# A cross-attention over 4096 tokens, its transfers issued by one queue in the order in which the program is written

## The chip, the cores and the metric

The kernel runs on one core of a Trainium2 chip. A core has five engines that each work through an instruction list of their own: TensorE (PE, matmuls), VectorE (DVE), ScalarE (ACT), GpSimd (POOL) and SyncE (SP). In this kernel SP does nothing but issue transfers (DMAs) from HBM to on-chip memory and back; ACT can issue them too, between its own arithmetic. The metric is the device time of one execution, in microseconds (us). Smaller is better.

## The reference

The network is a perceiver: a short sequence x (2 batches of 256 tokens, width 256) goes through twelve residual blocks, four of which attend to a long context `ctx_1024` (2 batches of 4096 tokens, width 256):

```python
x = x + _L0_xattn_ref(_layernorm(x), ctx_1024, mask, q_w, q_b, k_w, k_b, v_w, v_b)
x = x + _L0_attn_ref(_layernorm(x), w_down_q, w_down_kv, w_up_q, w_up_k, w_up_v, w_out, ...)
x = x + _L0_ffn_ref(...)
x = x + _L1_xattn_ref(_layernorm(x), ctx_1024, mask, Wq, Wk, Wv, Wo)
...
x = x + _L3_xattn_ref(_layernorm(x), ctx_1024, ctx_1024, Wq, Wk, Wv, Wp, focusing_factor)
...
```

The change is in the first block, L0_xattn, a masked softmax attention with 16 heads of 16 columns:

```python
q = split_heads(hidden @ q_w.T + q_b)       # 256 tokens a batch
k = split_heads(context @ k_w.T + k_b)      # 4096 tokens a batch
v = split_heads(context @ v_w.T + v_b)
scores = where(mask, -inf, q @ k.T / sqrt(16))
out = softmax(scores) @ v
```

One part of a later block is computed here as well, because it depends on the context alone. L3_xattn projects its keys from the context, takes absolute values and a softmax over logarithms, keeps the 11 largest of every 16 columns, and sums the products of the keys with the context. The kernel calls these keys the features, and does one batch of them during L0_xattn and the other during L1_xattn.

## The kernel before

**Units and steps.** `ContextAttention` (L805) cuts L0_xattn into 8 units, one for each of 2 batches and 4 chunks of heads (four heads in 128 partitions, 32 for each). `attend` (from L1090) is a loop over steps g = 0, 1, ...; a unit takes 16 steps (PER), so the stage has 128 first steps and some 20 more. A unit is passed over twice. In the first pass, `first_scores` (matmuls at L1257) multiplies queries by a tile of 512 keys, and DVE takes the row maxima (L1265, L1271). In the second, two steps and a whole unit later, `scores` (L1287) computes scores the other way round with the maximum already subtracted, ACT takes exp (L1296), and `weigh` (L1308) multiplies by the values. One step does one half of a key tile in each pass: 2 steps for 512 keys.

**Fills.** Between these, PE does what a planner (`plan`, from L947) has put into `fills[g]`: `project_keys` (matmuls k_ps at L1167), `project_values` (v_ps, through the helper at L242), projections of features (f_ps, L242 too), and their sums (kc_sum). Keys are projected in steps 0, 2, 5, 8, 12 and then about every fourth step; values in steps 1, 4, 6, 7, 9, 10 and so on; the sixteen halves of the features in steps 0, 3, 14, 16, 32, 33, 46, 49, 62, 65, 79, 80, 95, 97, 110 to 113 and 114. DVE's share of the features (the search for the eleven largest, L726 and L732, on the tile `fy`) is spread over the steps by the planner as well.

**How keys reach their tiles.** `project_keys(j)` works on a pair of context tiles of 512 tokens (`ctx_k`, loaded at L1149, 512 KB each). Its result in PSUM is copied by ACT into `k_dense` (L1177, two buffers, taken in turn). From there eight DMAs of 16 rows each (L1195, 32 KB each) move it into two of 14 key tiles (`xa_k`), four heads each to its own 32 partitions, and two small DMAs (L1185) put a row of the mask into each tile. Before the rows, `project_keys` issues the loads of the next pair of `ctx_k` (`load_keys_ctx`). The mask rows come from a table in HBM that the kernel writes itself at the start (L584, from `masks`, computed on DVE).

**Who issues.** Nearly everything is issued by SP. The exception is in this stage: for the first six pairs (`BY_ACT = 6`), the four rows of the pair's first tile are issued by ACT, the other four by SP (L1194, L1195). All transfers of the two queues take eight completion semaphores in turn, so a transfer's issue instruction first waits until the one eight before it has landed.

**Homes of the keys' context.** `ctx_k` has one pair of buffers (`bufs=1`, two tags). In L0_xattn there are more at the start: `SPARE = 3`, three pairs of value tiles (`xv`) that are not yet needed, which hold every second pair of context, so that two pairs can be there at a time until the sixth projection. For that the pool of value tiles is opened with the constructor of `ContextAttention` (L530 to L543).

**Values' context.** `load_values_ctx` (L1209) loads half a tile of context (`ctx_v`, 256 KB, four buffers); four are issued ahead of the loop, and each `project_values` issues one more.

**Features' context.** `Focus.load` (L752) fetches half a tile of context (`f_ctx`, 256 KB, two buffers). `Focus.start` issues the first; each projection of a half issues the next at its start (written ahead of its matmuls). `load_tokens` (L759) fetches the tokens for the sums (`f_tok`, 512 KB).

**The order of the work.** Within `context_attention` the engines in `by_program` (PE, DVE and ACT, L529) run their instructions in the order in which the Python program writes them (`tc.manual_schedule`). SP and POOL are not among them: a scheduler orders their instructions by its own estimates and may lift a transfer over others that are written before it.

**The start.** `center` and `inverse_root` (L335, L336: `rstd` on ACT, from the variance on DVE) normalise x; then queries are projected (`take_queries`), and the first pair of keys is projected ahead of them, with its rows and masks issued there. `self.beginning` is the rest of that: in step 0 it projects the second pair of keys (j = 1) ahead of the step's fills. `l0_attn` (from L1335), the next block, begins with the load of three of its weights (`L0a_wdq`, `L0a_wdkv`, `L0a_wuv`) into one tile of the pool of weights.

Of the kernel before, what the change touches and what calls it, by code (L numbers as in the profile page):

```python
# [21 lines left out]
F32 = mybir.dt.float32  # L22
# [6 lines left out]
P = 128  # L29
# [79 lines left out]
class Net:  # L109
# [52 lines left out]
    def load(self, *names, now=None):  # L162


        nc = self.nc
        t = self.weights.tile([P, 2048], F32, tag="w", name=f"w_{names[0]}")
        at, parts = 0, []
        for name in names:
            src = self.ins[name]
            n = int(np.prod(src.shape[1:]))  # L170
            letters = "abcde"[: len(src.shape) - 1]
            flat = src
            view = t[:, at : at + n]
            if len(letters) > 1:
# [343 lines left out]
    def context_attention(self, x, q_bias, k_bias, v_bias, wq, wk, values, layer, alive=None, block=None):  # L518

        tc = self.tc  # L529
        by_program = {mybir.EngineType.PE, mybir.EngineType.DVE, mybir.EngineType.Activation}  # L530
        to_values = lambda: tc.tile_pool(name="xa_v", bufs=1, reuse_waits="tile")
        with (
            tc.tile_pool(name="xa", bufs=1, reuse_waits="tile") as big,
            tc.tile_pool(name="xa_ctx", bufs=2, reuse_waits="tile") as cpool,
            to_values() if layer == 0 else nullcontext() as vpool,
        ):
            a = ContextAttention(self, layer, big, cpool, vpool, (wk, k_bias), v_bias)
            if layer == 0:
                for issue in self.postponed:
                    issue()  # L540
                a.load_keys_ctx()
                self.nc.sync.dma_start(out=self.vectors, in_=self.ins["vectors"])
                self.focus = Focus(self)  # L543
            a.wv, wo = values()
            if block is not None:
                with tc.manual_schedule(engines={mybir.EngineType.PE}), self.stage():
                    x = block(x, a.begin(3))
            with tc.manual_schedule(engines=by_program):
                return self.attend_to_context(a, x, q_bias, wq, wo, alive, nullcontext(vpool) if vpool else to_values())

    def attend_to_context(self, a, x, q_bias, wq, wo, alive, values):
# [9 lines left out]
        with (  # L561
            self.banks(mm=4, sc=2, acc=0),
            values as vpool,
            tc.tile_pool(name="xa_p", bufs=1, reuse_waits="tile") as ppool,
            tc.tile_pool(name="focus", bufs=2, reuse_waits="tile") as fpool,
        ):
            return a.attend(vpool, ppool, fpool, x, wo)
# [237 lines left out]
class ContextAttention:  # L805
# [7 lines left out]
    LAG = 2  # L813
    KEY_TILES = 14
    VALUE_TILES = 11
    BY_ACT = 6
    SPARE = 3

    def __init__(self, net, layer, big, cpool, vpool, keys, v_bias):
# [15 lines left out]
        self.spare = vpool is not None  # L835
        self.key_homes = {}
        if self.spare:
            self.vpool = vpool
            for n in range(self.SPARE):
                self.key_homes[2 * n + 1] = [self.new_values() for _ in range(2)]  # L840
# [249 lines left out]
    def attend(self, vpool, ppool, fpool, x, wo):  # L1090
# [3 lines left out]
        self.x, self.new = x, net.new_x()  # L1094
        if self.layer == 0:
            nc.gpsimd.memset(self.new[P // 2 :, ND - 1, S:], 0.0)
        for _ in range(4):
            self.load_values_ctx()
        focus.start(self.layer, fpool)
        fills = self.plan()  # L1100
        n = len(self.UNITS)

        rankings = {}
        for g in range((n + 1) * PER + LAG + 2):
            second = g - PER - LAG
            if 0 <= second < n * PER:
                self.scores(second // PER, second % PER)
            if g < n * PER:
                pair = self.first_scores(g // PER, g % PER)
            run(self.beginning)  # L1110
            if 1 <= g < n:
                self.finish_queries(g)
            if self.layer == 0:
# [5 lines left out]
                self.weigh((second - 1) // PER, (second - 1) % PER)  # L1119
            for fill in fills.get(g, ()):  # L1120
                fill()
            for kc in self.rankings.get(g, ()):
                if kc not in rankings:
                    y, _, factor = focus.chunks[kc]
                    rankings[kc] = focus.sparsify(fpool, y, factor)
                run(rankings[kc], 1)
# [5 lines left out]
                    self.finish(wo)  # L1132
            for kc in self.weighings.get(g, ()):
                run(focus.weighing[kc], 1)
        return self.new


    def load_keys_ctx(self):
        b, kc = next(self.key_loads, (None, None))
        if b is None:  # L1140
            return
        pair, homes = [], self.key_homes.pop(len(self.key_ctx), None)
        for i in range(2):
            if homes:
                flat = homes[i].rearrange("p k v -> p (k v)")[:, : ND * KC]
                ctx = flat.rearrange("p (d n) -> p d n", d=ND)
            else:
                ctx = self.cpool.tile([P, ND, KC], F32, name=f"ctx_k{i}", tag=f"ctx_k{i}", bufs=1)
            self.nc.sync.dma_start(out=ctx, in_=self.net.ins["ctxT"][b, kc + i])  # L1149
            pair.append(ctx)  # L1150
        self.key_ctx.append(pair)

    def project_keys(self, j, first, n=1):
# [25 lines left out]
            return  # L1179
        tiles = [self.key_tiles[(2 * j + i) % self.KEY_TILES] for i in range(2)]  # L1180

        def write_mask(i):
            rows = tiles[i].rearrange("(g r) n -> g r n", r=HP)
            mask = net.key_masks[self.layer, b * NKC + kc + i]
            nc.sync.dma_start(out=rows[:, DH + 1], in_=mask.unsqueeze(0).to_broadcast([NG, KC]))  # L1185

        if not self.spare or j != 2 * self.SPARE - 1:
            self.load_keys_ctx()
        for i, k in enumerate(tiles):
            if j > 0:  # L1190
                write_mask(i)
            queue = nc.scalar if self.spare and j < self.BY_ACT and i == 0 else nc.sync
            for g in range(NG):
                at = i * HR + g * DH  # L1194
                queue.dma_start(out=k[g * HP : g * HP + DH, :], in_=dense[at : at + DH, :])  # L1195
        if j == 0:
            for i in range(2):
                write_mask(i)

    def new_values(self):  # L1200
        return self.vpool.tile([P, KC // P, VW], F32, name="xv", tag="xv", bufs=self.VALUE_TILES)

    def load_values_ctx(self):
        b, kc, k2 = next(self.value_loads, (None, None, None))
# [7 lines left out]
    def project_values(self, b, kc, k2, first, n=1):  # L1212

        net, nc = self.net, self.nc
        if k2 == first == 0:
            v = self.new_values()
# [117 lines left out]

def l0_attn(net, x):  # L1335
    nc, tc = net.nc, net.tc
    wdq, wdkv, wuv = net.load("L0a_wdq", "L0a_wdkv", "L0a_wuv")
    wups = net.load("L0a_wuq", "L0a_wuk")
    wout = net.load("L0a_wout")
    g, be = net.vec("L0a_g"), net.vec("L0a_b")  # L1340
# [1469 lines left out]
```

## Time and profile before

| What | Value |
|---|---|
| Time, median of 3 runs | 2142.94 us (2139.47 to 2145.37) |
| The profiled execution: its own time | 2143.32 us |
| Its span in the trace | 2141.3 us |
| Mean granted clock of TensorE | 0.99 |
| PE / DVE / ACT busy, 0 to 24 us | 15.98 / 4.55 / 9.26 us |
| the same, 24 to 87 us (63 us; mean PEclk 0.92) | 54.04 / 42.01 / 15.63 us |
| the same, 87 to 200 us (113 us) | 111.52 / 96.58 / 76.76 us |
| the same, 200 to 620 us (420 us) | 414.93 / 338.13 / 289.51 us |
| Loads of `ctx_k` (512 KB each), whole kernel | 122 |
| Rows `xa_k<-k_dense` on SP's queue (32 KB each) | 488 |

Durations of single instructions come from the profiled execution, one run of the kernel under the hardware profiler; its own time is 2.0 us over its span. The span's rows are stretches of the trace: the busy time of each engine in the stretch, and PEclk, the clock that the throttle granted to TensorE as a share of full speed. Step 0 of the loop begins at 24.17 us and step 16 at 86.73 us; L0_xattn ends near 620 us. A line of the timeline of an engine holds start, duration, engine, line, operation, tiles and number of instructions that were put together; a bracket at its end gives the idle time ahead and what ended it. A line of the waits says which engine waited on which line, for what, and the total, the number and the longest of these waits. A line of the windows gives, for each engine, its busy time and instructions, then PEclk, the DMA engines' mean share and GB/s.

### The profile page before, as it was taken

To read this page: it belongs to the slowest core of one execution; us is meant where nothing else is said; L and a number is where in the kernel's file an instruction comes from. 1 tells how busy PE (TensorE), PEld (TensorE's weight loads), DVE (VectorE), ACT (ScalarE), POOL (GpSimd) and SP (SyncE) were. 2 spreads that over 40 slices of the span, in tenths; PEclk is the share of its full clock that TensorE was granted. 3 is DMA by queue.
4 is the path that set the end of the run, shared out by engine and by line. 5 is a ranking of instruction groups with operands and counts; after the bars stand their busy time and mean duration, and the time that the engine had idled before them with its cause. 6 is when DMAs were issued, how large, how long until landed. Compare 5 with 4: busy or idle time off the path is not lost.

```text
span 2141.3 us, 54941 instructions
## 1 busy us (share of the span) xinstructions
PE 2052.3 (96%) x21271; PEld 1119.4 (52%) x21271; DVE 1396.5 (65%) x5226; ACT 1119.0 (52%) x2319; POOL 448.6 (21%) x699
## 2 busy tenths in 40 slices
PE   8899999999998989999999999999999998998989
PEld 3355555555554454555555555654448554554444
DVE  4788888878757669888888787453342274445353
ACT  2367666667756453676666677432122273336161
POOL 4122122221207412221221122000011040015050
PEclk9999999999999999999999999999999999999999
DMA  6433333323112234333333230311223011102120
GB/s 231 123 111 102 103 106 111 105 91 93 39 51 94 69 124 137 113 98 112 107 119 107 77 106 25 106 38 59 99 98 118 20 32 35 40 32 53 67 53 25
DMA packets 105171, 183.71 MB, mean 86 GB/s; under 512 B 17632, under 2 KB 68128, under 8 KB 104016
## 3 DMA queue, kind: packets, MB, share of 16 engines
q1 hardware_dynamic: 103840, 179.12, 26.6%
q8 instruction: 169, 2.77, 0.5%
q10 hardware_dynamic: 1072, 1.08, 0.2%
q14 instruction: 90, 0.74, 0.1%
HBM read 152.74 MB, written 0.59 MB: 72 GB/s over the span
## 4 chain that ended last, share of the span: by engine, by line
PE 56%; DVE 4%; ACT 4%; issue 1%; DMA 0%; POOL 0%; SPq 0%; DVEq 0%; ACTq 0%; POOLq 0%
PE attn_acc L1308 6%; PE s L1287 6%; PE s L1257 5%; PE proj L235 5%; PE expert L235 3%; PE s L235 3%; PE c_acc L2065 3%; PE v_ps L242 3%; PE k_ps L1167 2%; PE ffn_ps L235 2%; PE s L1732 2%; ACT p L445 1%; PE v_ps L235 1%; PE moe_acc L1940 1%; PE kc_sum L242 1%; PE kq_ps L235 1%
## 5 line engine op out<-in xcount | busy, mean ns | idle before, releaser
L1296 ACT ACTIVATE p<-s 128x512 f32<-128x512 f32 (+1 forms) x768 | 512.0, 740 | 149.0 <-PE s L1287 147.3
L1265 DVE TENSOR_REDUCE mx<-s 128x1 f32<-128x512 f32 x512 | 329.6, 685 | 163.0 <-PE s L1257 160.6
L1271 DVE TENSOR_REDUCE mx<-s 128x2 f32<-128x1024 f32 x256 | 311.3, 1216 | 0.0
L1287 PE MATMUL s<-xa_q,xa_k 32*128 32x256 f32 x4096 | 298.0, 400 | 0.7 <-DVE mx L1265 0.7
L1257 PE MATMUL s<-xa_k,xa_q 32*128 32x512 f32 x2048 | 287.3, 602 | 11.2 <-ACT xv L1226 7.6
L1323 POOL TENSOR_TENSOR a<-a,more 128x256 f32<-128x256 f32 x210 | 153.0, 729 | 678.4 <-ACT more L1322 676.0
L1308 PE MATMUL attn_acc<-p,xv 128*32 128x256 f32 x4096 | 276.3, 385 | 5.4 <-ACT p L1296 3.7
L1287 PEld LDWEIGHTS s<-xa_q,xa_k 32*128 32x128 f32 x4096 | 188.4, 184 | 110.7 <-issue 50.6
L1308 PEld LDWEIGHTS attn_acc<-p,xv 128*32 128x32 f32 x4096 | 111.6, 109 | 227.0 <-ACT p L1296 163.4
L732 DVE MATCH_REPLACE8 fy<-least,fy 128x16 f32<-128x16 f32 x1024 | 162.5, 174 | 0.0
L1257 PEld LDWEIGHTS s<-xa_k,xa_q 32*128 32x128 f32 x2048 | 111.0, 185 | 44.5 <-issue 16.1
L464 POOL TENSOR_SCALAR p<-p,r 128x128 f32<-128x128 f32 (+1 forms) x192 | 88.7, 481 | 83.9 <-DVE r L460 64.8
L726 DVE MAX8 least<-fy 128x8 f32<-128x16 f32 x1024 | 96.9, 171 | 1.1
L1322 ACT COPY more<-attn_acc 128x256 f32<-128x256 f32 x210 | 79.0, 376 | 12.7 <-PE attn_acc L1308 10.7
L732 DVE MATCH_VALUE_LOAD fy<-least,fy 128x8 f32 x1024 | 83.4, 81 | 0.5
L1226 ACT COPY xv<-v_ps 128x512 f32<-128x512 f32 (+1 forms) x78 | 39.7, 510 | 78.7 <-PE v_ps L242 76.1
L445 ACT ACTIVATE p<-p,top 128x256 f32<-128x256 f32 (+1 forms) x128 | 56.7, 444 | 38.5 <-DVE top L433 33.5
L1167 PE MATMUL k_ps<-ctx_k,w_L1x_wq 128*32 128x256 f32 (+1 forms) x768 | 66.1, 460 | 0.0
L242 PE MATMUL kc_sum<-f_tok,fy 128*32 128x129 f32 (+2 forms) x1536 | 65.3, 309 | 0.0
L242 PE MATMUL v_ps<-w_L1x_wv,ctx_v 128*32 128x256 f32 x1024 | 62.7, 380 | 0.0
L242 PE MATMUL v_ps<-w_L0x_wv,ctx_v 128*32 128x256 f32 x1024 | 62.7, 380 | 0.0
L242 PE MATMUL f_ps<-f_wk,f_ctx 128*32 128x256 f32 x1024 | 62.1, 380 | 0.0
(501 smaller groups left out, 3096.7 us busy)
## 6 DMA issues: line engine op xcount, KB each, us to landing
ctx_k<-in_ctxT SPq DMA_DIRECT2D x122, 512.0 KB
ctx_v<-in_ctxT SPq DMA_DIRECT2D x64, 256.0 KB
xa_k<-k_dense SPq DMA_DIRECT2D x488, 32.0 KB
f_ctx<-in_ctxT SPq DMA_DIRECT2D x32, 256.0 KB
f_tok<-in_ctx SPq DMA_DIRECT2D x16, 512.0 KB
swapped<-raw SPq DMA_DIRECT2D x64, 128.0 KB
ctxT<-in_ctxT SPq DMA_DIRECT2D x16, 512.0 KB
ctx_n<-in_ctx SPq DMA_DIRECT2D x16, 512.0 KB
```

The costliest lines, as they stand in the source:

```text
L235: self.nc.tensor.matmul(out, lhsT=lhsT, rhs=rhs, start=i == 0, stop=i == len(pairs) - 1)
L242: self.nc.tensor.matmul(out[cols], lhsT=lhsT[:, cols], rhs=rhs, start=i == 0, stop=i == len(pairs) - 1)
L726: nc.vector.max(least[:, i], w)
L732: nc.vector.match_replace(w, least[:, i], w, 0.0)
L1167: nc.tensor.matmul(ps[row : row + HP, :], lhsT=self.wk[:, d, col : col + HP], rhs=ctx[:, d, at], start=d == 0, stop=d == ND - 1,)
L1257: nc.tensor.matmul(banks[i], lhsT=self.q[u][rows, qt * P : (qt + 1) * P], rhs=k[rows, :], start=True, stop=True,)
L1265: nc.vector.tensor_reduce(mx[:, qt, i : i + 1, kc], sc, AX.X, ALU.max)
L1271: nc.vector.tensor_reduce(mx[:, n % 2, 2:, n // 2], pair, AX.X, ALU.max)
L1287: nc.tensor.matmul(banks[i][:, kk * S : (kk + 1) * S], lhsT=k[rows, at], rhs=self.q[u][rows, :], start=True, stop=True,)
L1296: nc.scalar.activation(p[:, i : i + sc.shape[1], :], sc, AF.Exp, scale=DH**-0.5)
L1308: nc.tensor.matmul(acc[i * HP : (i + 1) * HP], lhsT=v[:, 2 * k2 + kk, at : at + HP], rhs=ps[:, i, kk * S : (kk + 1) * S], start=kk == 0, s ...
L1323: nc.gpsimd.tensor_tensor(self.adding, self.adding, more, ALU.add)
```

## The change

1. **SP in written order, in this block only.** For layer 0 SP joins `by_program`: its transfers are issued in the order in which the program writes them, from `attend_to_context` to the end of the block.
2. **Key rows by one queue.** All eight rows of a pair are issued by SP. For each of the two tiles its mask is written just ahead of its rows.
3. **One home for the keys' context.** The spare pairs in value tiles are gone: each pair goes into the two `ctx_k` buffers. The pool of value tiles is opened where the other layers open it.
4. **The first pair's rows** (j = 0) are kept back in `first_rows`, which `attend` calls after the first loads of values' and features' context; the order there is rows, masks, next context pair.
5. **Values' context** for layer 0: one load ahead of the loop and one in each of steps 0, 1 and 2, in place of four ahead of the loop.
6. **`run(self.beginning)`** (the second pair's projection in step 0) comes after the step's fills for layer 0, so PE's order there is first scores, features, keys.
7. **L0_attn's first weights** are loaded in step 32, by `load` with `touch=True`: ahead of each part's DMA, ACT copies one column of ones into it, so that the transfer is written after what ACT has done up to there. `l0_attn` takes the views from `net.first_of_l0_attn`.

DVE's order of instructions is the same in both kernels. `Focus.load` is not edited. The core of the diff:

```diff
     def load(self, *names, now=None, touch=False):
...
         for name in names:
+            if touch:
+                nc.scalar.copy(t[:, at : at + 1], self.ones[:, 0:1])
...
-        with (
-            tc.tile_pool(name="xa", bufs=1, reuse_waits="tile") as big,
-            tc.tile_pool(name="xa_ctx", bufs=2, reuse_waits="tile") as cpool,
-            to_values() if layer == 0 else nullcontext() as vpool,
-        ):
+        with tc.tile_pool(name="xa", ...) as big, tc.tile_pool(name="xa_ctx", ...) as cpool:
...
+            if layer == 0:
+                by_program.add(mybir.EngineType.SP)
             with tc.manual_schedule(engines=by_program):
...
-        for _ in range(4):
+        for _ in range(4 if self.layer > 0 else 1):
             self.load_values_ctx()
         focus.start(self.layer, fpool)
+        if self.layer == 0:
+            self.first_rows()
...
-            run(self.beginning)
+            if self.layer == 0 and g < 3:
+                self.load_values_ctx()
+            if self.layer > 0:
+                run(self.beginning)
...
             for fill in fills.get(g, ()):
                 fill()
+            run(self.beginning)
...
+        for g in range((n + 1) * PER + LAG + 2):
+            step(g)
+            if self.layer == 0 and g == 2 * self.ORDERED:
+                net.first_of_l0_attn = net.load("L0a_wdq", "L0a_wdkv", "L0a_wuv", touch=True)
...
-            if homes:
-                flat = homes[i].rearrange("p k v -> p (k v)")[:, : ND * KC]
-                ctx = flat.rearrange("p (d n) -> p d n", d=ND)
-            else:
-                ctx = self.cpool.tile([P, ND, KC], F32, name=f"ctx_k{i}", tag=f"ctx_k{i}", bufs=1)
+            ctx = self.cpool.tile([P, ND, KC], F32, name=f"ctx_k{i}", tag=f"ctx_k{i}", bufs=1)
...
-        if not self.spare or j != 2 * self.SPARE - 1:
-            self.load_keys_ctx()
-        for i, k in enumerate(tiles):
-            if j > 0:
-                write_mask(i)
-            queue = nc.scalar if self.spare and j < self.BY_ACT and i == 0 else nc.sync
-            for g in range(NG):
-                at = i * HR + g * DH
-                queue.dma_start(out=k[g * HP : g * HP + DH, :], in_=dense[at : at + DH, :])
-        if j == 0:
-            for i in range(2):
-                write_mask(i)
+        if self.layer == j == 0:
+            self.first_rows = lambda: (write_rows(0), write_rows(1), write_mask(0), write_mask(1), self.load_keys_ctx())
+            return
+        self.load_keys_ctx()
+        for i in range(2):
+            write_mask(i)
+            write_rows(i)
...
-    wdq, wdkv, wuv = net.load("L0a_wdq", "L0a_wdkv", "L0a_wuv")
+    wdq, wdkv, wuv = net.first_of_l0_attn
```

More of the change, by code (lines that the diff above doesn't have):

```diff
@@ L160, in sm, with load @@
         return self.small.tile([P, *shape], dtype, tag=tag or f"sm{n}", name=name)
-    def load(self, *names, now=None):
+    def load(self, *names, now=None, touch=False):
         nc = self.nc
@@ L530, in context_attention @@
         by_program = {mybir.EngineType.PE, mybir.EngineType.DVE, mybir.EngineType.Activation}
-        to_values = lambda: tc.tile_pool(name="xa_v", bufs=1, reuse_waits="tile")
-        with (
-            tc.tile_pool(name="xa", bufs=1, reuse_waits="tile") as big,
-            tc.tile_pool(name="xa_ctx", bufs=2, reuse_waits="tile") as cpool,
-            to_values() if layer == 0 else nullcontext() as vpool,
-        ):
-            a = ContextAttention(self, layer, big, cpool, vpool, (wk, k_bias), v_bias)
+        with tc.tile_pool(name="xa", bufs=1, reuse_waits="tile") as big, tc.tile_pool(name="xa_ctx", bufs=2, reuse_waits="tile") as cpool:
+            a = ContextAttention(self, layer, big, cpool, (wk, k_bias), v_bias)
             if layer == 0:
@@ L540, in context_attention @@
                     issue()
-                a.load_keys_ctx()
                 self.nc.sync.dma_start(out=self.vectors, in_=self.ins["vectors"])
@@ L547, in context_attention, with attend_to_context @@
                     x = block(x, a.begin(3))
+            if layer == 0:
+                by_program.add(mybir.EngineType.SP)
             with tc.manual_schedule(engines=by_program):
-                return self.attend_to_context(a, x, q_bias, wq, wo, alive, nullcontext(vpool) if vpool else to_values())
-    def attend_to_context(self, a, x, q_bias, wq, wo, alive, values):
+                return self.attend_to_context(a, x, q_bias, wq, wo, alive)
+    def attend_to_context(self, a, x, q_bias, wq, wo, alive):
         tc = self.tc
@@ L562, in attend_to_context @@
             self.banks(mm=4, sc=2, acc=0),
-            values as vpool,
+            tc.tile_pool(name="xa_v", bufs=1, reuse_waits="tile") as vpool,
             tc.tile_pool(name="xa_p", bufs=1, reuse_waits="tile") as ppool,
@@ L815, with __init__ @@
     VALUE_TILES = 11
-    BY_ACT = 6
-    SPARE = 3
-    def __init__(self, net, layer, big, cpool, vpool, keys, v_bias):
+    ORDERED = 16
+    def __init__(self, net, layer, big, cpool, keys, v_bias):
         self.net, self.nc, self.layer, self.cpool = net, net.nc, layer, cpool
@@ L834, in __init__ @@
             self.joined = Joined(net, big, lambda b, c: self.q[b * NC16 + c])
[L835 to L840, printed above, removed]
         self.begun, self.beginning = 0, iter(())
@@ L1103, in attend, with step @@
         rankings = {}
-        for g in range((n + 1) * PER + LAG + 2):
+        def step(g):
             second = g - PER - LAG
@@ L1141, in load_keys_ctx @@
             return
-        pair, homes = [], self.key_homes.pop(len(self.key_ctx), None)
+        pair = []
         for i in range(2):
-            if homes:
-                flat = homes[i].rearrange("p k v -> p (k v)")[:, : ND * KC]
-                ctx = flat.rearrange("p (d n) -> p d n", d=ND)
-            else:
-                ctx = self.cpool.tile([P, ND, KC], F32, name=f"ctx_k{i}", tag=f"ctx_k{i}", bufs=1)
+            ctx = self.cpool.tile([P, ND, KC], F32, name=f"ctx_k{i}", tag=f"ctx_k{i}", bufs=1)
             self.nc.sync.dma_start(out=ctx, in_=self.net.ins["ctxT"][b, kc + i])
@@ L1180, in project_keys, with write_rows @@
         tiles = [self.key_tiles[(2 * j + i) % self.KEY_TILES] for i in range(2)]
+        def write_rows(i):
+            for g in range(NG):
+                at = i * HR + g * DH
+                nc.sync.dma_start(out=tiles[i][g * HP : g * HP + DH, :], in_=dense[at : at + DH, :])
         def write_mask(i):
@@ L1185, in write_mask @@
             nc.sync.dma_start(out=rows[:, DH + 1], in_=mask.unsqueeze(0).to_broadcast([NG, KC]))
-        if not self.spare or j != 2 * self.SPARE - 1:
-            self.load_keys_ctx()
-        for i, k in enumerate(tiles):
-            if j > 0:
-                write_mask(i)
-            queue = nc.scalar if self.spare and j < self.BY_ACT and i == 0 else nc.sync
-            for g in range(NG):
-                at = i * HR + g * DH
-                queue.dma_start(out=k[g * HP : g * HP + DH, :], in_=dense[at : at + DH, :])
-        if j == 0:
-            for i in range(2):
-                write_mask(i)
-    def new_values(self):
-        return self.vpool.tile([P, KC // P, VW], F32, name="xv", tag="xv", bufs=self.VALUE_TILES)
+        if self.layer == j == 0:
[5 more added lines that the diff above has]
+            write_rows(i)
     def load_values_ctx(self):
@@ L1215, in project_values @@
         if k2 == first == 0:
-            v = self.new_values()
+            v = self.vpool.tile([P, KC // P, VW], F32, name="xv", tag="xv", bufs=self.VALUE_TILES)
             nc.gpsimd.memset(v, 1.0)
```

## The prediction

> **What bounds the kernel now.** I read the page first, then the waits of the first 100 us, then the timelines of PE, ACT and SP and the windows of the granted clock there. Unless another view is named, a time below is from a timeline of before, in us from the span's start; landing times are the trace's DMA completion events. The page says that PE is the bound over the whole:
>
> ```profile
> PE 2052.3 (96%) x21271; PEld 1119.4 (52%) x21271; DVE 1396.5 (65%) x5226; ACT 1119.0 (52%) x2319; POOL 448.6 (21%) x699
> ```
>
> So an edit pays only where PE stands still. The waits of 0 to 100 us (us in total, times, longest) show where that is in the changed stage:
>
> ```profile
> ACT fy L696 <- DMA xa_k<-k_dense: 11.0, 1, 11.0
> ...
> ACT fy L782 <- DMA xa_k<-k_dense: 10.1, 2, 5.8
> ...
> PE s L1257 <- ACT xv L1226: 7.6, 1, 7.6
> ...
> PE rstd_ps L235 <- ACT rstd L336: 2.8, 1, 2.8
> ...
> ACT rstd L335 <- DMA xa_k<-k_dense: 2.6, 1, 2.6
> ```
>
> ACT waits for key-row transfers that it issues itself. In the program every transfer takes one of eight semaphores in turn, so one more can only be issued when the eighth before it has landed; a four-row issue on ACT therefore stands behind 512 KB context loads. What PE does meanwhile, and after:
>
> ```profile
> 47.81 1.93 PE L242 MATMUL v_ps<-w_L0x_wv,ctx_v 128*32 128x256 f32 x32
> 49.67 1.14 PE L1257 MATMUL s<-xa_k,xa_q 32*128 32x512 f32 x8
> 50.74 1.93 PE L242 MATMUL v_ps<-w_L0x_wv,ctx_v 128*32 128x256 f32 x32
> 60.28 2.19 PE L1257 MATMUL s<-xa_k,xa_q 32*128 32x512 f32 x8 [7.60 <-ACT xv L1226]
> 62.40 3.64 PE L1167 MATMUL k_ps<-ctx_k,w_L0x_wk 128*32 128x512 f32 x16
> ```
>
> The reader should see 7.60 us of idle PE, and then matmuls at half speed (2.19 for 1.14, 3.64 for 1.92). The windows of one us tell why (PEclk is the third column from the end):
>
> ```profile
> 55.00:56.00 1.00, 0.00 (x0) 0.00 (x0) 0.00 (x0) 0.00 (x0) 0.00 (x0) 1.00 0.42 131
> 56.00:57.00 1.00, 0.00 (x0) 0.00 (x0) 0.00 (x0) 0.00 (x0) 0.00 (x0) 0.62 0.96 111
> 57.00:58.00 1.00, 0.00 (x0) 0.00 (x0) 0.00 (x0) 0.00 (x0) 0.00 (x0) 0.50 0.82 270
> ...
> 66.00:67.00 1.00, 1.00 (x12) 0.48 (x8) 0.00 (x0) 0.69 (x1) 0.00 (x0) 0.76 0.00 0
> ```
>
> PE stopped at 52.7, the clock was halved 3.7 us later, near 56.4, and came back near 66.5: 10.1 us, in which busy PE loses half. The idle 2.80 before 16.99 left PEclk at 1.00, so the drop lies somewhere between 2.8 and 3.7 us of idleness.
>
> From 100 to 620 us PE is as good as gapless: its timeline has no gap over 0.45 us. There the stage can only lose.
>
> **The change, part by part.** Steps are those of the loop in `attend`, g = 0, 1, ...; in the trace step 0 starts at 24.17 and step 16 at 86.73.
>
> *Start (removes).* ACT's first four issues go. They stand from 13.83 to 16.34, ahead of rstd (L335, 16.44), though var is ready at 12.37. Without them rstd ends near 12.95, and its PE work is next after q_ps, at 14.1 in place of 16.99: 2.9 us. What is late next? SP: in written order the mask store waits for DVE's masks (10.80), and behind it are two loads (0.65 each), eight rows (0.6 each, ACT's four among them) and two masks (0.55): issued by 18.4, the first mask landed by 19.2 (a mask lands 1.8 after issue). Queries would be ready at 24.17 - 2.9 = 21.3, so SP is hidden by 2 us. Gain 2.9.
>
> *Steps 0 to 16 (removes).* An undisturbed step is 2.93 (49.67 less 46.74, 75.00 to 77.93), step 0 is 5.39 (24.17 to 29.56). Sum 5.39 + 15 x 2.93 = 49.4; the trace took 62.56. The 13.2 that are over are the idle 7.60 and 1.36 (at 43.81), about 3.0 at the halved clock and 1.0 in step 2, all from ACT's waits. With no issue on ACT all of it goes.
>
> *One home for the keys' context (adds).* A pair of loads can start only when the last key projection has read its tiles. A pair issued at 100.47 landed 3.5 and 5.5 later; others took up to 5.9. Keys are projected in steps 0, 2, 5, 8, 12. Step 0's ends at 21.3 + 5.4 = 26.7, so the next pair lands at 30.4 and 32.3; step 2 starts at 29.6 and wants the second half after its scores (1.07) and two matmuls (0.45), at 31.1: 1.2 lost. For step 5 the pair waits on SP behind eight rows, two masks and three value loads, is issued near 36 and lands by 41.4, wanted at 33.6 + 2 x 2.93 + 1.5 = 41.0: 0.4 lost. Steps 8 and 12 are hidden (wanted 49.9 and 62, landed 49.5 and 59). Loss 1.6, bounds 0 and 2 x 5.9.
>
> *Value loads with the steps, key rows and masks in place.* Value loads stay four ahead. SP's hold per key pair: two context issues 0.85, two masks 1.1, eight rows at 0.6, and at the sixth row, the eighth transfer after the second context half, a wait till that has landed (at 160.05 for the pair of 154.18), after which three rows take 1.8: 7.6 from first to last, against 6.4 in before. Rows of the first tile land up to 0.6 later. In before, from the landing events, they are ahead of their first score by 3.4 us at the least (landed 255.0, used 258.4, step 56), so this is hidden; it costs if the rows come 3.4 later.
>
> *The feature context (moved).* This one the diff doesn't name. `Focus.load` is written at the start of one half chunk's projection and fetches for the next half. Before, the scheduler lifted it to where its buffer came free, a half chunk earlier; in written order it is issued only there, behind the key rows written before it. That is enough except where two halves stand in neighbouring steps with a key projection just ahead: steps 32/33 and 79/80. The first on SP, and on PE:
>
> ```profile
> 154.18 0.81 SPq L1149 DMA_DIRECT2D ctx_k<-in_ctxT  x2
> 155.07 5.50 SPq L1195 DMA_DIRECT2D xa_k<-k_dense  x8
> ```
> ```profile
> 157.51 1.93 PE L242 MATMUL f_ps<-f_wk,f_ctx 128*32 128x256 f32 x32
> ...
> 162.20 1.91 PE L242 MATMUL f_ps<-f_wk,f_ctx 128*32 128x256 f32 x32
> ```
>
> In this trace's clock the rows would be out at 154.18 + 7.6 = 161.8, the load lands 3.1 later (the f_ctx issued at 160.67 landed at 163.75), 164.9, and PE wants it at 162.20: 2.7 lost. At 358.06 the same sum with 7.1 (its context landed faster) gives 368.3 against 365.96: 2.3 lost. Neighbours 14/16 lose about 1.0, but DVE is full there (19.93 of 20 us in the window of 80 to 100) and covers it, say 0.1. Bounds: 0, if the rows get out faster, to 3 x 3.7.
>
> *L0_attn's weights and touch.* Three loads leave 54.25 to 55.8, where they stood between key rows, for about 150; they are wanted at 620. Three copies of one column on ACT, each no more than the 0.37 of the 256-column copies: at most 1.1, taken as 0.3.
>
> [...] Issues on ACT take 0.58 each, so eight rows on one queue cost 4 x 0.58 = 2.3 more than on two; yet four of ACT's took 6.78 from 51.78. [...]
>
> **Sum.** -2.9 - 13.2 + 1.6 + 2.7 + 2.3 + 0.1 + 0.3 = -9.1. The profiled execution took 2143.32 (span 2141.3), 0.4 over the median; from it 2134.2, from the median 2133.8. I forecast **2134.0**.
>
> **Rivals.** (a) The feature loads are in time after all: rows leave faster than 7.6, since fewer large loads are in flight. Then -9.1 - 5.0 = -14.1: 2129. For it: windows at 100 to 200 us show DMA busy 0.3 to 0.4. Against: the wait at the sixth row is for SP's own context pair, which nothing thins out. (b) Written order loses more at the start and in the pairs: the one-home wait costs the second half of its bounds (6 us) and all else stays: -3: 2140. For it: four of the first five key projections are close together. (c) Slower: SP's head holds the key rows past their first scores. Place: the eight pairs with margins under 6 us (steps 44, 56, 72, 104 to 112, 120, 124; 35.1 us together). Price: each delayed by a whole hold of 7.6 gives 8 x 7.6 - 35.1 = 25.7, less 9.1: +16.6, 2159. It decides from a mean delay of 5.5 (8 x 5.5 - 35.1 = 9). Against: no transfer written ahead of rows waits for later work. (d) It doesn't do what it says: ACT still waits, as k_dense has two buffers and its eviction needs the rows of two pairs before. Those land 7 us or more earlier in the sums above, so nothing; if not, the 13.2 come back and we are slower by 4: 2147.
>
> **How the numbers follow.** Forecast 0.45, (a) 0.17, (b) 0.24, (c) 0.08, (d) 0.06. The range takes the forecast, (a) and (b) with their bounds: 2127 to 2143, leaving out (c), (d) and a little of (a). 0.3% is 6.4 us, about what a measurement can tell from no change. Faster beyond it: the forecast and (a), 0.62; within: (b) and part of (d), 0.28; slower: (c) and part of (d), 0.10.
>
> **What would show it.** Right: rstd near 13, step 0 near 21.3, step 16 near 72.4, PEclk 1.00 from 40 to 70, PE gaps of over 2 us ahead of f_ps in steps 33 and 80, released by f_ctx. Wrong: PE gaps ahead of first scores in the steady steps, a halved clock after step 33, or step 16 later than 80.

## The result, and the profile after

The changed kernel takes 2157.5 us (median of 7 runs, 2149.86 to 2159.05); before took 2145.37 beside it (2139.47 to 2150.16). The ratio is 1.0052 (95% interval 1.0038 to 1.0066): 11 us slower, where 9 less were forecast. The profiled execution of after took 2157.74 with a span of 2155.7, so 14.4 are to be found between the two traces.

The page's line of busy time (engine, us, share of the span, instructions) hardly differs from before: PE is busy 8.7 us more, with the same number of matmuls.

```profile
PE 2061.0 (96%) x21271; PEld 1121.7 (52%) x21271; DVE 1396.5 (65%) x5226; ACT 1119.6 (52%) x2322; POOL 449.1 (21%) x699
```

The two largest waits of PE in 0 to 640 us of after that before did not have (us in total, times, longest):

```profile
PE f_ps L244 <- DMA f_ctx<-in_ctxT: 10.5, 3, 5.1
PE k_ps L1165 <- DMA ctx_k<-in_ctxT: 5.6, 3, 2.8
```

The waits of PE for xv and fy, which came from ACT's issuing, are gone; in their place PE waits for context. Its timeline has the six places, ahead of the keys of steps 2, 5 and 8 and of the features of steps 16, 33 and 80; five of them are these (start, us, line, operation, and in brackets the idle time ahead and its releaser), and step 16 follows below:

```profile
32.85 1.91 PE L1165 MATMUL k_ps<-ctx_k,w_L0x_wk 128*32 128x512 f32 x12 [0.73 <-DMA ctx_k<-in_ctxT]
...
44.46 3.09 PE L1165 MATMUL k_ps<-ctx_k,w_L0x_wk 128*32 128x512 f32 x16 [2.76 <-DMA ctx_k<-in_ctxT]
...
56.60 4.33 PE L1165 MATMUL k_ps<-ctx_k,w_L0x_wk 128*32 128x512 f32 x16 [2.11 <-DMA ctx_k<-in_ctxT]
...
164.81 2.45 PE L244 MATMUL f_ps<-f_wk,f_ctx 128*32 128x256 f32 x32 [2.24 <-DMA f_ctx<-in_ctxT]
...
373.06 2.49 PE L244 MATMUL f_ps<-f_wk,f_ctx 128*32 128x256 f32 x32 [3.14 <-DMA f_ctx<-in_ctxT]
```

Steps 2, 5 and 8 take 4.75, 6.92 and 7.51 us, where an undisturbed step takes 2.93: together 10.4 more, and that is all by which steps 0 to 16 exceed 49.4. The steps are matched by PE's order of instructions, which is the same in both from step 1 on. How far after lies behind before (us, from the timelines):

| Point in before | after - before | since the last |
|---|---|---|
| step 0, 24.17 | -2.6 | -2.6 |
| step 16, 86.73 | -5.3 | -2.8 |
| 100 | -0.05 | +5.3 |
| 175, behind step 33 | +4.3 | +4.3 |
| 300 | +3.9 | -0.4 |
| 480, behind step 80 | +8.9 | +5.0 |
| 610, end of the block's sums | +9.0 | 0.1 |
| 619, normalization of the next block | +10.7 | +1.7 |
| end of the span | +14.4 | +3.7 |

PE's timeline of after around step 16:

```profile
82.47 0.44 PE L1230 MATMUL top_ps<-ident,xa_top 128*128 128x128 f32 x2
87.98 1.93 PE L244 MATMUL f_ps<-f_wk,f_ctx 128*32 128x256 f32 x16 [5.08 <-DMA f_ctx<-in_ctxT]
89.84 1.68 PE L1252 MATMUL s<-xa_k,xa_q 32*128 32x512 f32 x8
```

The largest single wait stands in step 16, not in 33 or 80 where the prediction put its two. Why the transfer is late is read from SP's timeline:

```profile
61.07 1.03 SPq L1147 DMA_DIRECT2D ctx_k<-in_ctxT  x2
62.20 0.55 SPq L1188 DMA_DIRECT2D xa_k<-key_masks  x1
62.84 2.88 SPq L1183 DMA_DIRECT2D xa_k<-k_dense  x4
65.81 0.52 SPq L1188 DMA_DIRECT2D xa_k<-key_masks  x1
68.18 3.15 SPq L1183 DMA_DIRECT2D xa_k<-k_dense  x4
71.43 1.96 SPq L1204 DMA_DIRECT2D ctx_v<-in_ctxT  x3
73.48 1.02 SPq L1147 DMA_DIRECT2D ctx_k<-in_ctxT  x2
...
83.77 0.61 SPq L1204 DMA_DIRECT2D ctx_v<-in_ctxT  x1
84.42 0.61 SPq L750 DMA_DIRECT2D f_ctx<-in_ctxT  x1
```

From one pair of contexts to the next SP needs 12.4 us (61.07 to 73.48); PE wants a pair every three to four steps, 8.8 to 11.7. So SP falls behind, and what is written in step 14 (76.60) leaves at 84.42. In the middle of a pair's rows SP stands still until 68.18: by the landing events the first of its own two contexts landed at 68.16, and it is the eighth transfer before that row. By SP's waits in 24 to 90 us it stood 10.5 us in all, in eight places, for such contexts. For PE to free the one home it stood long only once, 4.2 us ahead of the pair of 27.10, which is the pair that step 2 waits for.

### The profile page after: what moved, and what is told of

It is laid out like the page before. It is cut to its first block, busy times and chain, and to the rows that moved or that the text cites. A ratio compares the mean times of both kernels' runs of the same rounds, so it can differ in the third digit from the quotient of the medians.

```text
span 2155.7 us, 54903 instructions
## 1 busy us (share of the span) xinstructions
PE 2061.0 (96%) x21271; PEld 1121.7 (52%) x21271; DVE 1396.5 (65%) x5226; ACT 1119.6 (52%) x2322; POOL 449.1 (21%) x699
## 4 chain that ended last, share of the span: by engine, by line
PE 56%; DVE 5%; ACT 3%; issue 1%; DMA 1%; POOL 0%; SPq 0%; DVEq 0%; ACTq 0%; POOLq 0%
PE attn_acc L1303 6%; PE s L1282 6%; PE s L1252 5%; PE proj L237 5%; PE expert L237 3%; PE s L237 3%; PE c_acc L2060 3%; PE v_ps L244 3%; PE k_ps L1165 2%; PE ffn_ps L237 2%; PE s L1727 2%; PE v_ps L237 1%; ACT p L447 1%; PE moe_acc L1935 1%; PE qk_ps L237 1%; PE kc_sum L244 1%
## 5 line engine op out<-in xcount | busy, mean ns | idle before, releaser
L1252 PEld LDWEIGHTS s<-xa_k,xa_q 32*128 32x128 f32 x2048 | 110.3, 186 | 35.0 <-issue 18.1
L1317 ACT COPY more<-attn_acc 128x256 f32<-128x256 f32 x210 | 79.0, 376 | 11.7 <-PE attn_acc L1303 10.7
L1165 PE MATMUL k_ps<-ctx_k,w_L0x_wk 128*32 128x256 f32 (+1 forms) x752 | 69.0, 465 | 5.7 <-DMA ctx_k<-in_ctxT 5.6
L244 PE MATMUL f_ps<-f_wk,f_ctx 128*32 128x256 f32 x1024 | 64.1, 389 | 10.5 <-DMA f_ctx<-in_ctxT 10.5
L244 PE MATMUL v_ps<-w_L1x_wv,ctx_v 128*32 128x256 f32 x1024 | 62.7, 380 | 0.0
```

What stands on the lines that cost most here:

```text
L244: self.nc.tensor.matmul(out[cols], lhsT=lhsT[:, cols], rhs=rhs, start=i == 0, stop=i == len(pairs) - 1)
L1165: nc.tensor.matmul(ps[row : row + HP, :], lhsT=self.wk[:, d, col : col + HP], rhs=ctx[:, d, at], start=d == 0, stop=d == ND - 1,)
L1252: nc.tensor.matmul(banks[i], lhsT=self.q[u][rows, qt * P : (qt + 1) * P], rhs=k[rows, :], start=True, stop=True,)
```

## The experiments

All stage times are from one profile each; each ratio is to runs of before on the same chip, and since the chip differs between some rows, kernels are compared with each other by their ratios or by their traces. "Steps 0-16" is the time from the first scores of step 0 to those of step 16 (62.56 in before, 59.78 in after; 49.4 would be undisturbed). "Half clock" is for how long of them PEclk stood at 0.50 (10.24 in before); a busy PE loses half of that (the 16 matmuls of a key projection took 3.64 us in before's half clock and 1.92 at full clock), and the clock differs between executions of one kernel (last section), so differences of 1 to 2 us between two stage times say little. "End" is how far the block's end (610 us) lies from before's.

| Kernel | steps 0-16 | half clock | end | median | ratio (interval) |
|---|---|---|---|---|---|
| after | 59.78 | 3.41 | +9.0 | 2157.50 | 1.0052 (1.0038 to 1.0066) |
| e1 features early | 57.67 | 3.41 | -7.0 | 2140.44 | 0.9986 (0.9977 to 0.9995) |
| e2 free order | 57.76 | 3.41 | -7.5 | 2136.00 | 0.9963 (0.9951 to 0.9975) |
| e3 two homes | 56.23 | 3.41 | +1.7 | 2147.73 | 1.0021 (1.0010 to 1.0032) |
| e4 before, rows by SP | 56.50 | 3.41 | -8.1 | 2136.38 | 0.9967 (0.9955 to 0.9979) |
| e5 early, two ahead | 57.38 | 6.83 | -6.7 | 2137.26 | 0.9971 (0.9961 to 0.9981) |
| e6 early, rows by ACT | 57.72 | 3.41 | -2.9 | 2143.03 | 0.9996 (0.9984 to 1.0008) |
| e7 early, rows first | 75.05 | 17.07 | +27.7 | 2178.31 | 1.0160 (1.0141 to 1.0178) |
| e8 early, weights at start | 56.64 | 0 | -8.0 | 2138.96 | 0.9980 (0.9967 to 0.9993) |
| e9 e5 without masks | 50.55 | 0 | -13.9 | 2131.51 | 0.9942 (0.9924 to 0.9959) |
| e10 e5, rows first | 54.27 | 0 | -9.9 | 2142.12 | 0.9985 (0.9973 to 0.9997) |
| e11 e5, tokens late | 56.58 | 6.83 | -7.8 | 2137.70 | 0.9968 (0.9950 to 0.9986) |
| e12 e5, masks by GpSimd | 54.02 | 3.41 | -10.9 | 2132.34 | 0.9948 (0.9930 to 0.9966) |
| e13 e5, masks by ACT | 54.76 | 3.41 | -9.7 | 2136.68 | 0.9966 (0.9953 to 0.9978) |
| e14 e5, rows by ACT | 55.79 | 3.41 | -9.1 | 2137.22 | 0.9971 (0.9956 to 0.9985) |

### Is it the place of the feature loads? (e1, e2)

```diff
# e1, in Focus.project, for L0_xattn
-            if t % 2 == 0:
+            if self.b > 0 and t % 2 == 0 or kc == t == 0:
                 self.load()
...
+        if self.b == 0 and (first + n) % 2 == 0:
+            self.load()
```

> The changed kernel, but in L0_xattn each load of features' context (f_ctx) is written at the end of the projection two halves before its use, a half earlier than now; nothing else moves. Theory A (the written order puts f_ctx behind the key rows): the idle 5.08, 2.24 and 3.14 us ahead of f_ps in steps 16, 33 and 80 go, with the halved clock behind each: 10 us in all at that loop's end at the least, up to 18, so 2140 to 2147 against 2157.5. Theory B (SP is full anyway, since it issues all rows and waits for each context pair): the load moves its wait to the next context pair, the gain is under 5 us, 2153 or more.

Theory A holds: 2140.44, 17 less than after by the medians and 14 by the ratios. From step 16 to the end of the block e1 keeps its distance to before (-7.2 at step 16, -7.0 at the end), so the three waits of steps 16, 33 and 80, and all that followed them, were the place of one load. Its waits of PE in 0 to 640 us name no f_ps any more; those of k_ps for contexts remain:

```profile
PE k_ps L1167 <- DMA ctx_k<-in_ctxT: 3.7, 4, 2.6
```

```diff
# e2
-            if layer == 0:
-                by_program.add(mybir.EngineType.SP)
```

> The changed kernel, but SP is left to the scheduler as before; one home, one queue for the rows and all else stay. Theory A (the written order is what costs): no wait for f_ctx in steps 16, 33, 80, only the waits for ctx_k in steps 2, 5, 8 remain: about 2143. Theory B (one queue and one home cost): 2152 or more, with the idle time still ahead of k_ps and f_ps in the first 17 steps.

Theory A again, and better than forecast: 2136.0. With the scheduler's order the rest of the change brings 7 us. The written order takes them away and 11 more, by the place of that one load: e1 keeps the written order, and at the block's end it and e2 lie within 0.5 us of each other.

### The two terms that should have paid (e4)

```diff
# e4, in the kernel before
-    BY_ACT = 6
+    BY_ACT = 0
```

> The kernel before, but all eight rows of each pair are issued by SP and none by ACT; scheduler's order, spare homes and loads as before. My prediction's first two terms alone: rstd 2.9 us earlier and no stall of ACT in steps 0 to 16, 16 us less, about 2129. Theory B (one queue for the rows is itself dear): SP's extra issues (24 at 0.6) delay context or rows, and the gain is under 8 us, 2137 or more.

Half came: 2136.38, 7 less than before by the medians and 8 in the stage, not 16. Step 0 starts 2.0 earlier and ACT's stalls are gone, but step 0 takes 4.9 longer. PE's timeline of e4:

```profile
23.89 1.92 PE L1167 MATMUL k_ps<-xv,w_L0x_wk 128*32 128x512 f32 x16
29.16 3.38 PE L242 MATMUL f_ps<-f_wk,f_ctx 128*32 128x256 f32 x32 [3.34 <-DMA f_ctx<-in_ctxT]
```

The first f_ctx is issued at 23.27 there, behind eight rows, two masks and three value loads. The step-by-step gain of the prediction had been taken as if only ACT's waits stood between 62.6 and 49.4; with ACT free, the next late transfer shows.

### Home, order and issuer of the keys (e3, e5, e6, e7)

```diff
# e3
-            ctx = self.cpool.tile([P, ND, KC], F32, name=f"ctx_k{i}", tag=f"ctx_k{i}", bufs=1)
+            ctx = self.cpool.tile([P, ND, KC], F32, name=f"ctx_k{i}", tag=f"ctx_k{i}", bufs=2 if self.layer == 0 else 1)
```

> The changed kernel, but the keys' context has two pairs of buffers in L0_xattn, in place of one. Theory A: the idle 0.73, 2.76 and 2.11 us ahead of k_ps in steps 2, 5 and 8 goes, and the half clock behind step 8 with it: 6 to 9 us less, about 2150; the waits for f_ctx stay. Theory C (it is not the home but SP, which issues the pair late behind rows that wait for the pair before): the pair is issued no earlier, and under 2 us are gained.

The size (10 less than after by the medians, 7 by the ratios) fits theory A, the place does not. Step 2 loses its wait (2.93) and step 8 nearly all of it (3.78 in place of 7.51), but step 5 takes 8.92 (6.92 in after): the pair is written at the same place and issued only 0.7 earlier there (36.39 and 37.08), as theory C said. Of the gain, 5 come in steps 33 and 80. The idle ahead of f_ps falls there from 2.24 and 3.14 to 1.69 and 1.88, as f_ctx leaves earlier; the rest is the clock, which after these shorter gaps stayed at 1.00.

```diff
# e5 = e1 and two buffers as in e3, and the pair two projections ahead
                     issue()
+                a.load_keys_ctx()
                 self.nc.sync.dma_start(out=self.vectors, in_=self.ins["vectors"])
```

> The first experiment's kernel (features' loads a half earlier), and in L0_xattn two pairs of buffers for the keys' context, loaded two projections ahead (the first two pairs ahead of the loop). Theory A/C: what is left in steps 2, 5 and 8 comes from context that is issued one projection ahead, behind the rows and three value loads, and lands too late; two ahead all three waits for ctx_k go and the halved clock too: 5 to 9 us less than 2140, about 2133. Rival (the transfers of the first 60 us are bounded by bandwidth): the same bytes come in the same time, the wait moves to v_ps or to the first scores, gain under 2 us.

The rival's half came true: no wait for ctx_k is left, at step 9 e5 is 14.5 ahead of before, and then PE waits 5.36 for a value load in step 11. Steps 0 to 16 take 57.38, as in e1. Its SP timeline, and after it PE's:

```profile
39.05 1.03 SPq L1150 DMA_DIRECT2D ctx_k<-in_ctxT  x2
...
50.95 1.42 SPq L1150 DMA_DIRECT2D ctx_k<-in_ctxT  x2
...
53.14 2.47 SPq L1186 DMA_DIRECT2D xa_k<-k_dense  x4
...
57.23 3.33 SPq L1186 DMA_DIRECT2D xa_k<-k_dense  x4
60.67 1.31 SPq L1207 DMA_DIRECT2D ctx_v<-in_ctxT  x2
```
```profile
63.87 3.64 PE L244 MATMUL v_ps<-w_L0x_wv,ctx_v 128*32 128x256 f32 x32 [5.36 <-DMA ctx_v<-in_ctxT]
```

The value load leaves at 60.67; PE would have used it at 58.5. Between the pairs lie 11.9 us.

```diff
# e6 = e1, in write_rows
+            queue = nc.scalar if self.layer == 0 and j < 6 and i == 0 else nc.sync
...
-                nc.sync.dma_start(out=tiles[i][...], in_=dense[...])
+                queue.dma_start(out=tiles[i][...], in_=dense[...])
```

> The first experiment's kernel, but ACT issues the four rows of the first tile of the first six pairs again, as before the change. My theory (ACT stands behind the eighth transfer before): ACT's copies wait for issues again, PE idles behind xv or k_dense, 8 to 14 us more than 2140: about 2150. Theory B (SP's issue time of 0.6 a row bounds the first steps): SP is relieved of 2.4 us a pair, contexts come earlier, and it is 3 to 7 us faster, about 2135.

Neither: 2143.03, a ratio 0.0010 above that of e1. At the block's end e6 is 4.1 behind e1, and all of it from the start, where step 0 begins 4.1 later (ACT issues the first rows at 22.0, behind its copies of the queries). In steps 0 to 16 the two are equal (57.72, 57.67): there ACT's four issues took 2.4 to 3.3, so its long waits of before (6.78 from 51.78) belong to before's order, not to the issuer alone.

```diff
# e7 = e1, in project_keys (e10: the same in e5)
-        self.load_keys_ctx()
         for i in range(2):
             write_mask(i)
             write_rows(i)
+        self.load_keys_ctx()
```

> The first experiment's kernel, but the load of the next pair of contexts is written behind the masks and rows of the pair in place of ahead of them. If SP's hold comes from the wait of the sixth and later transfers for that context, rows leave in 6 us without a wait; the context is issued 6 us later, though, in steps 2, 5, 8 where it is late already: the waits for ctx_k grow from 3.7 us to 10 or more, about 2147. If rows that wait were the bound, it would be faster than 2140.

The direction is right and the size far off: 2178.31. With one home a context that is issued 6 us later is late in 15 projections over the whole block:

```profile
PE k_ps L1167 <- DMA ctx_k<-in_ctxT: 23.6, 15, 6.2
```

### The weights (e8)

```diff
# e8 = e1
-            if self.layer == 0 and g == 2 * self.ORDERED:
-                net.first_of_l0_attn = net.load("L0a_wdq", "L0a_wdkv", "L0a_wuv", touch=True)
...
-    wdq, wdkv, wuv = net.first_of_l0_attn
+    wdq, wdkv, wuv = net.load("L0a_wdq", "L0a_wdkv", "L0a_wuv")
```

> The first experiment's kernel, but the three weights of the next block are loaded by that block's own code, without the touch; the scheduler then issues them among the first loads of the kernel. My term for the touch was 0.3 us. If it is that small, this run differs by what 0.75 MB more at the start cost, 0 to 2.5 us more than 2140; if the weights in step 32 and the touch cost more than 2 us, it is faster than 2138.

2138.96 against 2140.44 for e1, with intervals that overlap: where the weights are loaded makes no difference that these runs tell. The three copies of the touch take 0.36 us on ACT in after's trace.

### What bounds steps 0 to 16? (e9 to e14)

```diff
# e9 = e5
         for i in range(2):
-            write_mask(i)
+            if self.layer > 0:
+                write_mask(i)
             write_rows(i)
```

> The fifth experiment's kernel without the mask rows of L0_xattn's key tiles from the second pair on, so the mask is left out of those scores: ten transfers fewer in steps 0 to 16, hardly any bytes. What holds steps 0 to 16 at 57.4 us (49.4 undisturbed) there is one of two. Theory C (the number of transfers that SP issues in order, at 0.6 us or by eight in flight): 10 x 0.6 = 6 us fewer are in the way of the late value load, the wait of 5.4 us ahead of v_ps in step 11 goes, steps 0 to 16 take about 51, the time is 2130 to 2133. Theory D (bytes: the DMA engines carry no more in that time): steps 0 to 16 stay at 57, the time at 2137.

Theory C: 50.55 for steps 0 to 16, 1.1 over the undisturbed 49.4, and 2131.51. Ten transfers of 8 KB were worth 6.8 us. Of these 4.3 are idle time ahead of the values of step 11 (1.11 in place of 5.36); the rest is the clock, at half speed for 6.83 us in e5 and not at all here. SP's distance from pair to pair falls to 8.4 and 9.9:

```profile
38.10 1.02 SPq L1150 DMA_DIRECT2D ctx_k<-in_ctxT  x2
39.22 5.83 SPq L1186 DMA_DIRECT2D xa_k<-k_dense  x8
...
46.53 1.91 SPq L1150 DMA_DIRECT2D ctx_k<-in_ctxT  x2
48.55 6.38 SPq L1186 DMA_DIRECT2D xa_k<-k_dense  x8
55.03 1.30 SPq L1208 DMA_DIRECT2D ctx_v<-in_ctxT  x2
56.42 1.89 SPq L1150 DMA_DIRECT2D ctx_k<-in_ctxT  x2
```

The value load of step 11 leaves at 55.03 in place of 60.67. That is 5.6 earlier, though only six of the ten masks stood ahead of it, 3.3 us of issue time.

> The fifth experiment's kernel, but the pair of contexts (needed two projections later) is written behind the masks and rows. Theory C': what costs SP is the wait in the middle of a pair's rows for the contexts written just ahead of them (2.2 and 1.3 us at 43.6 and 46.4 in the fifth); with the contexts behind, rows leave in 6 us and the value load of step 11 comes 3 to 5 us earlier: steps 0 to 16 about 53, 2133. If the wait just passes to the transfers behind the contexts (the eighth in turn is then a value load or the next rows): 57 as before, 2137. Since the contexts are two ahead, the loss of the seventh experiment must not come back.

In the stage as theory C' said, in part: 54.27, with a wait of 3.0 ahead of v_ps in place of 5.4, after which the clock did not fall. The loss of e7 did not come back, since the contexts are two ahead. The median (2142.12) does not show the gain; that is looked at below.

```diff
# e11 = e5; load_tokens is no longer called in Focus.project for kc == 0
+            if self.layer == 0 and g == 16:
+                focus.load_tokens()
```

> The fifth experiment's kernel, but the first load of tokens (f_tok, 512 KB, first used by kc_sum some 60 us later) is written in step 16 in place of step 0. It takes one transfer and 512 KB out of the stretch. Theory D (bytes): 512 KB at the 266 KB per us of the window from 20 to 30 us, some 2 us off the wait of 5.4 in step 11. Theory C (number): 0.6 us off. Both small, told apart in the trace and not by the time: 2135 or 2137.

Steps 0 to 16 shorten by 0.8 for 512 KB and one transfer, the wait of step 11 by 0.6 (4.77 in place of 5.36), as theory C has it and not the 2 of theory D. Bytes are not what bounds them.

```diff
# e12 = e5, in write_mask (e13: nc.scalar in place of nc.gpsimd; e14: the rows as in e6, for 0 < j < 6)
+            queue = nc.gpsimd if self.layer == 0 and 0 < j < 6 else nc.sync
-            nc.sync.dma_start(out=rows[:, DH + 1], in_=mask...)
+            queue.dma_start(out=rows[:, DH + 1], in_=mask...)
```

> The fifth experiment's kernel, all of the computation kept, but GpSimd issues the masks of pairs 1 to 5, on its own queue and with its own semaphores. Takes ten issues from SP and ten places of the eight semaphores, as the run without masks did: steps 0 to 16 about 51 in place of 57.4, 2131 to 2133. If GpSimd's issue is slow or late, first scores wait for masks and it is 2137 or more.

> The same with ACT as the issuer: SP's issues fall by ten, but the masks still take their turns of the eight semaphores shared by SP and ACT. If SP's issue time is the bound: 51 us for steps 0 to 16, as with GpSimd. If the eight in flight are the bound: 57 as before, or more where ACT stands behind one.

> The fifth experiment's kernel with the four rows of the first tile of pairs 1 to 5 issued by ACT (the first pair's stay on SP, which cost 4 us at the start in the sixth). Twenty issues less on SP, none less of the eight semaphores' turns. Issue time the bound: under 52 for steps 0 to 16, 2131. Eight in flight the bound: 56 or more, 2137.

Ten masks off SP bring 3.4 us (GpSimd, 54.02) or 2.6 (ACT, 54.76), not 6.8; twenty rows off SP bring 1.6 (55.79). In idle time of PE in these steps it is less, 3.18, 3.46 and 4.54 us in place of 5.36; the rest is again the clock. With ACT the old stall is back, here in e14's waits and in ACT's timeline:

```profile
PE s L1256 <- ACT xv L1225: 3.2, 1, 3.2
```
```profile
46.37 4.30 ACTq L1187 DMA_DIRECT2D xa_k<-k_dense  x4
50.72 1.15 ACT L695 ACTIVATE fy<-fy,eps 128x1024 f32<-128x1024 f32 x1 [6.66 <-DMA xa_k<-k_dense]
```

So SP's issue time and the ten turns of the semaphores do not explain all of e9's gain: e12 takes both off SP and still stands in its rows (8.79 us for eight from 48.82, 6.38 in e9), waiting for contexts that landed 7.1 and 8.7 us after their issue. Why those took longer than e9's 6.0 and 6.3 stays open. e12 keeps the whole computation and has the lowest median of those that do: 2132.34, ratio 0.9948 to before, though its interval overlaps that of e2.

## Why the prediction was wrong, point by point

- **Start, -2.9:** right. rstd is free of ACT's issues, step 0 starts 2.6 earlier.
- **Steps 0 to 16, -13.2, and one home, +1.6:** wrong, and the first failure. Together -2.8 came for -11.6. "With no issue on ACT all of it goes" held for ACT's waits; what failed is the term for late contexts, 1.6, which measured 10.4. Step 2 lost 1.8 (1.2 forecast; this one is the home's, for in e3 it is gone), step 5 lost 4.0 (0.4), and step 8, taken as hidden, 4.6, its half clock included. For step 5 the place was right, near 36 (37.08), but the pair landed 7.2 and 7.9 after its issue and not 5.4. The same transfers had to leave SP, at 0.6 each and eight in flight. The prediction worked out SP's hold of a pair (7.6 us, from a pair that stood alone at 154) and never set it beside the interval at which PE wants pairs. In the busy stretch, from the pair of 37.08 on, the distance is 11.7 to 12.4, and PE wants a pair every 8.8 to 11.7. So SP's queue (its issues, their order and its waits for landings together) became the bound; e9, which takes ten transfers off it and brings 50.55, shows that. Which of the three counts for how much stays open, and so does why contexts took 6.8 to 8.3 us to land there and not 3.5 to 5.9. Value loads had been issued just ahead of them, but in e9 the pair of 38.10, behind three value loads too, landed after 3.9 and 5.8.
- **Feature loads behind key rows, +2.7 and +2.3:** the mechanism was right, and it is what makes after slower (e1, e2). The idle was 2.24 and 3.14, close to both; the sizes were +4.3 and +5.0, since the clock fell to half after each, which the prediction had not priced. e3, whose gaps there were shorter and left the clock at 1.00, lost 2.1 in each.
- **Steps 14 and 16, +0.1 (about 1.0 late, covered by a full DVE):** wrong, the second failure: +5.3. SP was 8 us behind by then, so the load came 5.08 late; and the cover was not one. DVE is full there, but its work waits for PE's scores: in 80 to 92 us of after DVE's wait for the first scores was 5.2 us. An engine that is fed by the one that stands still stands still too.
- **Touch, +0.3:** right in size (0.36 on ACT, no wait behind it).
- **Later parts, 0:** after adds 1.7 at the block's end and 3.7 beyond it; the granted clock shows 3.3 of these 5.4 (last section).
- **Rivals.** (c) has after's time to 2 us but not its place: no first scores waited for key rows. (b) named the stretch and gave it 6 us more than the sum; it took 8.8 more, and (b) had nothing for step 16. (a) is what e1 brought about by moving the load, without the other waits going. (d) is refuted. The waits do name k_dense as waiting for rows, at 60.98 and 72.80, but k_ps ended at those moments (60.93 and 72.7), and the rows of two pairs before had landed at 48.79 and 61.00; the view names the event that came last.
- Of the signs given, the gaps in steps 33 and 80, released by f_ctx, were there; PEclk was not 1.00 from 40 to 70, and step 16 began at 81.4, past the 80 named as a sign of error.

## What to carry to other kernels

When transfers move from two issuers to one in written order, add up that issuer's time over the busiest stretch (transfers x issue time, 0.6 us each here, and the wait for the eighth before, with the landing times of that stretch, here 6.8 to 8.3 us for a context) and compare it with the pace at which the consumer asks, before crediting any stall that goes. In written order a load stands where it is written: look for every load that was written late because a scheduler used to lift it, and write it one use earlier. A stall's price was here its idle time and the half clock behind it (4.3 us for 2.24 idle, 5.0 for 3.14), and a full engine hid nothing where the stalled one fed it (5.2 us of waiting on DVE in step 16).

## What was not expected of the hardware

The clock. The prediction read from before that a gap of 2.8 us leaves PEclk at 1.00 and that the drop needs more. In after it was halved behind idle gaps of 2.11 (ahead of 56.60), 2.24 and 3.14, and not behind one of 2.76 (41.70 to 44.46). So the prediction's bound of 2.8 to 3.7 us of idleness was a misreading. These are the windows of one us of after in which the clock changes (start:end, us, busy time of PE, PEld, DVE, ACT, POOL, then PEclk, DMA share, GB/s):

```profile
56.00:57.00 1.00, 0.40 (x2) 0.17 (x4) 1.00 (x2) 0.00 (x0) 0.00 (x0) 0.93 0.11 39
60.00:61.00 1.00, 1.00 (x9) 0.14 (x8) 0.00 (x0) 0.02 (x1) 0.00 (x0) 0.87 0.14 33
87.00:88.00 1.00, 0.02 (x3) 0.05 (x4) 0.00 (x0) 0.00 (x0) 0.00 (x0) 0.79 0.80 247
166.00:167.00 1.00, 1.00 (x16) 0.31 (x7) 0.00 (x0) 0.00 (x0) 0.00 (x0) 0.54 0.91 360
374.00:375.00 1.00, 1.00 (x20) 0.50 (x12) 0.00 (x0) 0.00 (x0) 0.00 (x0) 0.65 0.00 0
623.00:624.00 1.00, 0.99 (x3) 0.80 (x4) 0.15 (x1) 0.00 (x0) 0.00 (x0) 0.73 0.00 0
```

A window in which the clock goes from 1 to 0.5 at time t has the mean 1 - 0.5 x (end - t). So the drops lie at 56.86, 87.58, 166.08, 374.30 and 623.46, and the first return (0.5 to 1) at 60.26: 3.40 later. The second drop came within its gap, 4.68 after PE had stopped at 82.90. The first, third and fourth came 0.26, 1.27 and 1.24 after PE had begun again behind their gaps (56.60, 164.81, 373.06), and the fifth 0.45 behind a gap of 1.02 that ended at 623.01, among short matmuls at the block's end. In before the mean of 0.62 in 56 to 57 us puts the drop at 56.24, 3.56 after PE had stopped at 52.68. Gaps behind which the clock stayed at 1.00 were 2.76 in after (PEclk 1.00 from 39 to 48 us), 2.80 in before (14.19 to 16.99) and 3.0 in e10, all longer than the 2.11 and 2.24 behind which it fell. So in these traces the length of a gap does not tell whether the clock falls behind it; what decides it, no run here shows.

Beyond the block the kernels drift too. From 610 us on nothing is edited, but one minus PEclk, summed over windows of 10 us, gives 18.1 us in before, 21.4 in after, 14.7 in e1, 22.8 in e10 and 24.9 in e12. After loses 5.4 to before from there on (1.7 at the block's end and 3.7 beyond it), of which the sums show 3.3. In its profile e10 goes from 9.9 ahead of before at 610 to 0.9 behind it at 2100, 10.8 of which the sums show 4.7, and e12 from 10.9 ahead to 2.7, 8.2 of which they show 6.8. Where the rest comes from stays open.

The granted clock differs between executions of one kernel too. After's seven runs go from 2149.86 us with a mean granted clock of 0.989 (2151.02 with 0.991) to 2159.05 with 0.986; e12's eight go from 2126.48 with 0.994 to 2140.88 with 0.987. The profiles of e10 and e12 are of their slowest runs, so these drifts are not those of the median: e12's is 11 below before's, all that its stage gains, while e10's is 1.6 below (ratio 0.9985), so there most of the gain is lost. That the clock has this part in the drifts is read from the sums and from these clocks; no run here changes the clock alone.
